# Decoder block on one core: keys projected ahead of queries in the linear-only steps, first loads reordered, the last linear output and its neighbours moved in the hand-written order

## The chip, the cores and the metric

One core of a Trainium2 chip. The metric is the device time of the kernel in microseconds (us). It was run three times: 1145.2, 1141.48 and 1145.28 us, median 1145.2.

## The reference

The kernel computes one pre-norm decoder layer on x (32 sequences, 128 tokens, 256 features) in fp32, with 16 heads of 16 features:

```
x = x + linear_attention(layernorm(x))        # causal; phi(q), phi(k) with phi = elu + 1
x = x + cross_attention(layernorm(x), ctx)    # softmax attention on a given context
x = x + ffn(layernorm(x))                     # silu(W1 x) * (W2 x), gelu(H1 .), gelu(H2 .), W3
```

In the linear attention, the weight of key s for query t is phi(q_t) . phi(k_s) for s <= t, and the sum is divided by the sum of the weights. The feed-forward widths are 256 to 1024 to 1024 to 1024 to 256, with ternary weights and one scale for each output.

## The kernel before

**Stages.** The 32 sequences are handled as 16 pairs. A step m (`step`, L660) works on the linear attention of pair m ("a_" units) and on the cross attention of pair m - 3 ("b_" units). Steps 0 to 2 use the list `first` (L621), in which only a_ units and the preparation of the first b_ pairs run; steps 3 to 15 use `both`; steps 16 and 17 use `alone` (L646), in which the linear attention is finished but for the tail of pair 15; step 18 uses `last`, step 19 uses `rest`. Then eight blocks of four sequences go through the feed-forward network (L771).

**Order.** Each list is an order written out by hand. A unit issues its instructions on TensorE (PE), VectorE (DVE), ScalarE (ACT) and GpSimd (POOL), and each engine executes what it was given in the order of the lists. SyncE (SP) issues most loads. An engine that has to wait for an operand therefore holds up everything listed behind it on that engine.

**The units that matter.** `a_queries` (L473) projects queries on PE (L359), then `phi` (L457) takes exp (L463) and relu (L465) on ACT and combines them on DVE (L467) in place in the buffer e; `masked` (L377) then makes two parity-masked copies, `qa2`, on POOL (L381), which read e. `a_keys` (L470) does the same into a buffer of its own, `ka`, with no masked copies. The buffers e and r exist once (`bufs=1`, L460 and L461). Only pair 0 has a separate e for its queries. `a_scores` (L487) multiplies keys and masked queries on PE (L388) into the two score buffers and applies the causal mask on DVE (L494). `a_weighted` (L502, PE L404, ACT copy L412), `a_divide` (L505, PE transposes L419, DVE L423 to L428), `a_turn` (L508, PE L512, ACT L514) and `a_out` (L517, PE L367, DVE addition to x L519) follow. `a_norm` and `b_norm` (L445, L524) take statistics on DVE (L134 to L143), twelve small instructions of a Newton iteration on POOL (L146 to L149) and two normalising instructions on POOL (L339). PE's small outputs share four PSUM banks in rotation (`bank`, L328).

**Fills.** In the tail of the attention, feed-forward work of block 0 is put between attention units. The list `fills` (L682) holds eleven pieces: the transposed input, eight gates (two products of 4 matmuls each, L229) and the first two of eight gelu chunks (16 matmuls each, L239). The unit `beside` (L631) starts one fill on PE, `settle` (L638) issues what follows it on ACT, DVE and POOL, and then reloads the exp table (L83). Both do nothing until the last linear output, `(a_out, 15, 1)`, is issued (L668).

**First loads.** `load_w` (L282) loads one of seven 256 KB projection weights; L287 to L302 write out which queue issues which and in what order: 0 to 3 are the query, key, value and output weights of the linear attention, 4 to 6 the query, key and value weights of the cross attention.

Of the kernel before, what the change touches and what calls it, by code (L numbers as in the profile page):

```python
# [26 lines left out]
NPAIR = B // 2  # L27
# [19 lines left out]
def decoder_block_kernel(  # L47
# [14 lines left out]
    nc = tc.nc  # L62
# [19 lines left out]
    def load_exp():  # L82
        nc.scalar.activation(warm, zero, AF.Exp)  # L83
# [172 lines left out]
    def pool(stack, name, bufs, **kw):  # L256
        return stack.enter_context(tc.tile_pool(name=name, bufs=bufs, **kw))
# [4 lines left out]
    with tc.manual_schedule(engines=ORDERED):  # L262
# [15 lines left out]
        def load_x(count):  # L278
            for _, n in zip(range(count), loads):
                nc.sync.dma_start(out=xs[n], in_=x[2 * n : 2 * n + 2].rearrange("b s d -> s b d"))  # L280

        def load_w(queue, n):  # L282
            queue.dma_start(
                out=WA[:, n] if n < 4 else WB[:, n - 4], in_=wattn[n].rearrange("(c p) o -> p c o", p=P)
            )
# [2 lines left out]
        load_w(nc.scalar, 5)  # L288
        load_x(1)
        nc.sync.dma_start(out=cT0, in_=ctxT[:, : 2 * S].rearrange("(c p) t -> p c t", p=P))  # L290
        load_w(nc.scalar, 6)
        nc.scalar.dma_start(out=col, in_=cols)
        load_w(nc.sync, 0)
        load_w(nc.scalar, 1)
        load_exp()
        load_x(1)
        load_w(nc.sync, 2)
        nc.sync.dma_start(out=row, in_=rows.partition_broadcast(P))
        load_w(nc.sync, 3)
# [304 lines left out]
        def b_divide(m, j):  # L604
# [14 lines left out]
            (b_scores, 0, 1), (a_weighted, 0, 1), (a_out, 0, 0), (a_norm, 2), (a_values, 1), (b_load, 2),  # L619
        ]  # L620
        first = [  # L621
            (a_scores, 0, 0), (a_norm, 2), (a_turn, -1, 1), (a_queries, 1), (a_out, -1, 1), (b_norm, 2),
            (a_weighted, 0, 0), (a_bias, 0), (a_scores, 0, 1), (a_divide, 0, 0), (a_keys, 1),
            (b_transpose, 1), (a_values, 1), (a_weighted, 0, 1), (a_turn, 0, 0), (a_bias, 1),
            (b_queries, 1), (a_transpose, 2), (a_out, 0, 0), (a_divide, 0, 1), (b_load, 2),
        ]
# [11 lines left out]
        def settle():  # L638
# [4 lines left out]
                load_exp()  # L643
            begun.clear()

        alone = [  # L646
            (b_load, 2), (b_maxima, 0, 0), settle, (b_weighted, -1, 1), (a_divide, -1, 1), (b_transpose, 1),
            (b_values, 1), (b_turn_maxima, 0, 0), (b_divide, -1, 1), (a_turn, -1, 1),
            (b_queries, 1), (b_scores, 0, 0), (a_out, -1, 1), beside, (b_norm, 2),
            (b_maxima, 0, 1), settle, (b_weighted, 0, 0), beside,  # L650
            (b_turn_maxima, 0, 1), (b_divide, 0, 0), settle, (b_keys, 1), (b_scores, 0, 1), beside,
        ]
        last = [
            (b_maxima, 0, 0), settle, (b_weighted, -1, 1), beside, (b_turn_maxima, 0, 0), (b_divide, -1, 1),
            settle, (b_scores, 0, 0), beside, (b_maxima, 0, 1), settle, (b_weighted, 0, 0), beside,
            (b_turn_maxima, 0, 1), (b_divide, 0, 0), settle, (b_scores, 0, 1), beside,
        ]
        rest = [(b_weighted, -1, 1), settle, beside, (b_divide, -1, 1), settle]

        def step(m):  # L660
            b = m - SKEW
            units = (
                first if m < prologue else both if m < NPAIR
                else alone if b < NPAIR - 1 else last if b < NPAIR else rest
            )
            for unit in units:
                if unit in (beside, settle):
                    if (a_out, NPAIR - 1, 1) in done:  # L668
                        unit()
                    continue  # L670
                f, ahead, *j = unit
                n = ahead + (b if f.__name__.startswith("b_") else m)
                if 0 <= n < NPAIR and (f, n, *j) not in done:
                    done.add((f, n, *j))
                    f(n, *j)
                    if (f, n, *j) == (a_out, NPAIR - 1, 1):
                        right.close()
                        hid["r"] = pool(ffn, "hr", 1, side="right", reuse_waits="tile")
# [7 lines left out]
        done = {(a_norm, 0), (a_norm, 1), (a_transpose, 1)}  # L686
# [21 lines left out]
        for m in range(NPAIR + SKEW + 1):  # L708
            waiting = None
            if m >= prologue and spare:  # L710
                n = spare.pop(0)
                dst = (W1, W2, H1)[FFN_SLICES[n][0]]
                load(n, dst)
                waiting = again(lambda: stages.tile([P, TB], F32, tag="stage", name="stage"), n)
            step(m)
            if waiting:
                test(dst, *waiting)
            if m == NPAIR - 1:
                block["xn"] = ffn_norm(0, nc.gpsimd)
# [217 lines left out]
```

## Time and profile before

| what | value |
|---|---|
| three runs | 1145.2, 1141.48, 1145.28 us |
| the profiled execution | 1142.26 us, of which the span from the first to the last instruction is 1140.2 us |
| granted TensorE clock, mean | 0.993 |
| start and step 0 (0 to 35.1 us) | PE busy 27.5 us of 35.1 |
| step 1 (35.1 to 52.85 us) | PE busy 15.3 us of 17.75 |
| step 2 (52.85 to 70.9 us) | PE busy 17.3 us of 18.05 |
| step 3 (70.9 to 99.5 us) | PE busy 28.2 us of 28.6 |
| step 16 with its fills and the start of step 17 (447.1 to 471.8 us) | PE busy 22.3 us of 24.7 |
| 471.8 us to 503.0 us | PE busy 30.0 us of 31.2 |

Starts are in us from the beginning of the span. A row of the timeline gives start, length, engine, line, operation, output and inputs, the count, and in brackets how long the engine was idle before it and what ended that wait. In the windows view each row gives the busy time of each engine in a stretch and the TensorE clock that was granted; 1.00 is full and 0.50 half.

### The profile page before, as it was taken

How to read it: one execution, taken by the hardware profiler on the slowest of the kernel's cores; microseconds unless marked ns; L12 is line 12 of the kernel's file. 1: busy time of each engine (PE TensorE's matmuls, PEld its weight loads, DVE VectorE, ACT ScalarE, POOL GpSimd, SP SyncE). 2: the span in 40 equal slices, each digit the busy share in tenths (PEclk: the TensorE clock that was granted, in tenths of full speed). 3: DMA queues.
4: the chain of work that ended last, by engine and by line, in shares of the span. 5: the costliest groups of instructions: out<-in, count | busy, mean ns of one | idle time of the engine just before them, and what ended most of it. 6: DMA issues, size and time to landing. Idle time of an engine off the chain costs nothing.

```text
span 1140.2 us, 20344 instructions
## 1 busy us (share of the span) xinstructions
PE 1118.8 (98%) x8238; PEld 904.3 (79%) x8238; DVE 576.7 (51%) x1296; ACT 411.9 (36%) x655; POOL 446.9 (39%) x1025
## 2 busy tenths in 40 slices
PE   8899999999999998999999999999999999999998
PEld 6677777777777776778888888888888888888887
DVE  6567777777777777452243443432522522522411
ACT  3344444444444444882231221321311311312311
POOL 4455555555555545455231231321311411412311
PEclk9899999999999999999999999999999999999999
DMA  8001111111111100005001111000000000000000
GB/s 273 1 20 48 48 47 48 48 47 48 47 48 48 47 11 11 1 2 185 17 22 37 38 38 37 19 14 5 24 10 5 19 1 1 20 1 10 9 1 22
DMA packets 26548, 39.28 MB, mean 34 GB/s; under 512 B 2512, under 2 KB 18640, under 8 KB 26448
## 3 DMA queue, kind: packets, MB, share of 16 engines
q1 hardware_dynamic: 21456, 25.57, 6.6%
q0 software_dynamic: 4032, 11.54, 3.1%
q8 instruction: 67, 1.10, 0.4%
q10 hardware_dynamic: 960, 0.81, 0.2%
q14 instruction: 33, 0.27, 0.1%
HBM read 33.71 MB, written 4.19 MB: 33 GB/s over the span
## 4 chain that ended last, share of the span: by engine, by line
PE 92%; DVE 3%; ACT 2%; POOL 1%; issue 1%; DMA 0%; SPq 0%; POOLq 0%; DVEq 0%
PE ph L218 50%; PE pp L359 9%; PE py L757 5%; PE pf L404 5%; PE pv L367 4%; PE se L388 3%; PE sa L388 3%; PE pw L367 3%; PE sm L388 3%; PE po L419 3%; PE pt L349 1%; DVE at L494 1%; PE se L588 1%; DVE nm L565 1%; PE pz L574 1%
## 5 line engine op out<-in xcount | busy, mean ns | idle before, releaser
L181 DVE TENSOR_TENSOR gl<-hg,gh 128x512 fp32r<-128x512 f32 x126 | 87.2, 692 | 347.0 <-POOL gh L180 344.0
L180 POOL CAST gh<-hg 128x512 fp32r<-128x512 f32 x128 | 79.1, 618 | 362.4 <-ACT hg L242 362.4
L242 ACT ACTIVATE hg<-ph,col 128x512 f32<-128x512 f32 x128 | 88.3, 690 | 363.0 <-PE ph L218 363.0
L218 PE MATMUL ph<-sh,H 128*128 128x512 f32 x512 | 199.5, 390 | 0.0
L218 PE MATMUL ph<-sl,H 128*128 128x512 f32 x512 | 199.2, 389 | 0.0
L218 PE MATMUL ph<-gh,H 128*128 128x512 f32 x512 | 199.2, 389 | 0.0
L218 PE MATMUL ph<-gl,H 128*128 128x512 f32 x512 | 199.2, 389 | 0.0
L218 PEld LDWEIGHTS ph<-sh,H 128*128 128x128 f32 x512 | 96.1, 188 | 20.4 <-issue 0.5
L218 PEld LDWEIGHTS ph<-gl,H 128*128 128x128 f32 x512 | 96.1, 188 | 19.9
L218 PEld LDWEIGHTS ph<-gh,H 128*128 128x128 f32 x512 | 96.1, 188 | 19.9
L218 PEld LDWEIGHTS ph<-sl,H 128*128 128x128 f32 x512 | 96.1, 188 | 19.9
L218 PE MATMUL ph<-xh,W 128*128 128x512 f32 x256 | 100.6, 393 | 0.0
L218 PE MATMUL ph<-xl,W 128*128 128x512 f32 x256 | 99.8, 390 | 0.0
L180 POOL CAST sh<-hs 128x512 fp32r<-128x512 f32 x64 | 58.5, 914 | 68.8 <-DVE hs L234 60.4
L565 DVE TENSOR_REDUCE nm<-sm 128x8 f32<-128x1024 f32 x64 | 75.2, 1216 | 16.9 <-PE sm L388 16.9
L494 DVE TENSOR_TENSOR at<-sa,causal 128x1024 f32<-128x1024 f32 x64 | 75.2, 1215 | 6.2 <-PE sa L388 6.1
L232 ACT ACTIVATE sil<-ph,col 128x512 f32<-128x512 f32 x64 | 44.1, 690 | 74.9 <-PE ph L218 74.8
L146 POOL TENSOR_TENSOR t<-rstd 128x2 f32<-128x2 f32 x138 | 32.5, 236 | 90.8 <-DVE hv L143 83.6
L234 DVE SCALAR_TENSOR_TENSOR hs<-ph,col,sil 128x512 f32<-128x512 f32 x64 | 48.0, 750 | 36.4 <-PE ph L218 20.2
L598 ACT ACTIVATE pr<-se 128x1024 f32<-128x1024 f32 x64 | 62.0, 1022 | 12.0 <-PE se L588 11.9
L757 PE MATMUL py<-W,gh 128*128 128x256 f32 x256 | 62.6, 285 | 0.0
L757 PE MATMUL py<-W,gl 128*128 128x256 f32 x256 | 62.0, 283 | 0.0
(133 smaller groups left out, 1937.7 us busy)
## 6 DMA issues: line engine op xcount, KB each, us to landing
x<-in_x_dram SPq DMA_DIRECT2D x16, 256.0 KB, 5.5
cT<-in_ctxT_dram SPq DMA_DIRECT2D x16, 256.0 KB, 2.6
stage<-in_h1T_dram SPq DMA_DIRECT2D x16, 256.0 KB, 2.9
H<-in_h1T_dram POOLq DMA_DIRECT2D x8, 512.0 KB, 3.6
H<-in_h2T_dram POOLq DMA_DIRECT2D x8, 512.0 KB, 7.1
out_dram<-y SPq DMA_DIRECT2D x32, 128.0 KB, 1.7
raw<-in_h2T_dram SPq DMA_DIRECT2D x16, 256.0 KB, 2.7
stage<-in_w1T_dram SPq DMA_DIRECT2D x4, 256.0 KB, 4.2
```

What stands on the lines that cost most here:

```text
L180: (high_engine.copy if high_engine is nc.scalar else high_engine.tensor_copy)(high, t)
L181: lows.append(lambda: low_engine.tensor_tensor(low, t, high.bitcast(F32), ALU.subtract))
L218: nc.tensor.matmul(pp, lhsT=w[:, k, ts(c, P)], rhs=parts[p], start=(k == 0 and p == 0), stop=(k == len(src) - 1 and p == 1),)
L242: nc.scalar.activation(t, pp, AF.Gelu, scale=col[:, c_scale + c : c_scale + c + 1])
L359: nc.tensor.matmul(pp[:, c, :], lhsT=w[:, d, ts(c, P)], rhs=src[:, d, :], start=(d == 0), stop=(d == DC - 1))
L367: nc.tensor.matmul(pp, lhsT=src[:, d, :], rhs=w[:, d, :], start=(d == 0), stop=(d == DC - 1))
L388: nc.tensor.matmul(sc[g // 2][:, g % 2, 2 * c : 2 * c + 2, :], lhsT=loaded[32 * g : 32 * g + 32, c, ts(j, S)], rhs=streamed[32 * g : 32 * ...
L404: nc.tensor.matmul(pf[32 * g : 32 * g + 32, i, :], lhsT=v[:, 4 * i + g, :], rhs=weights[g // 2][:, g % 2, i, :], start=True, stop=True,)
L494: nc.vector.tensor_tensor(at.rearrange("p g i s -> p (g i) s"), sc[u].rearrange("p g i s -> p (g i) s"), causal.unsqueeze(1).to_broadcast( ...
L565: nc.vector.tensor_reduce(nm[:, 2 * u : 2 * u + 2, :], sc[u], AX.X, ALU.max, negate=True)
L598: nc.scalar.activation(pr, sc[u], AF.Exp)
L757: nc.tensor.matmul(py[:, :D], lhsT=h[k][p][:, ts(j, S)], rhs=W3[:, k, :], start=(k == 0 and p == 0), stop=(k == HC - 1 and p == 1),)
```

## The change

Three things are moved, and no arithmetic is added or removed.

1. First loads: weight 6 (cross values) and weight 1 (linear keys) are issued by SP instead of ACT, weight 1 after the second x tile.
2. In `first`, `a_keys` of the next pair takes the place of `a_queries` and the other way round.
3. Step 16 has a list of its own, `begins`, in which the last `a_turn` and `a_out` come ahead of `b_queries`, and there is one more `beside` after `b_scores`. `alone`, now for step 17 only, loses the units that do nothing there. The test that kept fills back until the last linear output is dropped, because the list itself now puts it first. With the additional place in step 16, the eleven fills are used up in step 18, and the place in `rest` finds none.

```diff
         load_w(nc.scalar, 5)
         load_x(1)
         nc.sync.dma_start(out=cT0, in_=ctxT[:, : 2 * S].rearrange("(c p) t -> p c t", p=P))
-        load_w(nc.scalar, 6)
+        load_w(nc.sync, 6)
         nc.scalar.dma_start(out=col, in_=cols)
         load_w(nc.sync, 0)
-        load_w(nc.scalar, 1)
         load_exp()
         load_x(1)
+        load_w(nc.sync, 1)
         load_w(nc.sync, 2)
...
         first = [
-            (a_scores, 0, 0), (a_norm, 2), (a_turn, -1, 1), (a_queries, 1), (a_out, -1, 1), (b_norm, 2),
-            (a_weighted, 0, 0), (a_bias, 0), (a_scores, 0, 1), (a_divide, 0, 0), (a_keys, 1),
+            (a_scores, 0, 0), (a_norm, 2), (a_turn, -1, 1), (a_keys, 1), (a_out, -1, 1), (b_norm, 2),
+            (a_weighted, 0, 0), (a_bias, 0), (a_scores, 0, 1), (a_divide, 0, 0), (a_queries, 1),
             (b_transpose, 1), (a_values, 1), (a_weighted, 0, 1), (a_turn, 0, 0), (a_bias, 1),
             (b_queries, 1), (a_transpose, 2), (a_out, 0, 0), (a_divide, 0, 1), (b_load, 2),
         ]
...
+        begins = [
+            (b_load, 2), (b_maxima, 0, 0), (b_weighted, -1, 1), (a_divide, -1, 1), (b_transpose, 1),
+            (b_values, 1), (b_turn_maxima, 0, 0), (a_turn, -1, 1), (b_divide, -1, 1), (a_out, -1, 1), beside,
+            (b_queries, 1), (b_scores, 0, 0), beside,
+            (b_norm, 2), (b_maxima, 0, 1), settle, (b_weighted, 0, 0), beside,
+            (b_turn_maxima, 0, 1), (b_divide, 0, 0), settle, (b_keys, 1), (b_scores, 0, 1), beside,
+        ]
         alone = [
-            (b_load, 2), (b_maxima, 0, 0), settle, (b_weighted, -1, 1), (a_divide, -1, 1), (b_transpose, 1),
-            (b_values, 1), (b_turn_maxima, 0, 0), (b_divide, -1, 1), (a_turn, -1, 1),
-            (b_queries, 1), (b_scores, 0, 0), (a_out, -1, 1), beside, (b_norm, 2),
+            (b_maxima, 0, 0), settle, (b_weighted, -1, 1), (b_transpose, 1), (b_values, 1),
+            (b_turn_maxima, 0, 0), (b_divide, -1, 1), (b_queries, 1), (b_scores, 0, 0), beside,
             (b_maxima, 0, 1), settle, (b_weighted, 0, 0), beside,
             (b_turn_maxima, 0, 1), (b_divide, 0, 0), settle, (b_keys, 1), (b_scores, 0, 1), beside,
         ]
...
-                else alone if b < NPAIR - 1 else last if b < NPAIR else rest
+                else begins if m == NPAIR else alone if b < NPAIR - 1 else last if b < NPAIR else rest
             )
             for unit in units:
                 if unit in (beside, settle):
-                    if (a_out, NPAIR - 1, 1) in done:
-                        unit()
+                    unit()
                     continue
```

## The prediction

> **What bounds the kernel now.** I read the page first: its busy times, and the row of the granted clock.
>
> ```profile
> PE 1118.8 (98%) x8238; PEld 904.3 (79%) x8238; DVE 576.7 (51%) x1296; ACT 411.9 (36%) x655; POOL 446.9 (39%) x1025
> ...
> PEclk9899999999999999999999999999999999999999
> ```
>
> PE is busy for 1118.8 of 1140.2 us, and no matmul is added or removed. So the change can only win from PE's 21 us of idle time and from stretches at a reduced clock: slice 2 (28.5 to 57 us) has the one 8 in the row of the clock, and a shorter stretch, too short for this row, appears below at 455.6 us. Both lie in edited steps. Next the waits of the whole run:
>
> ```profile
> ACT e L463 <- POOL qa L381: 17.2, 3, 6.2
> ...
> PE pt L349 <- ACT r L465: 3.9, 2, 2.1
> PE pz L574 <- DVE z L570: 2.3, 2, 2.0
> ```
>
> Three times, once in each linear-only step, ACT stands before the exp of the keys until POOL has read e for the masked queries: e exists once. The timeline of step 0 shows what this does to PE:
>
> ```profile
> 27.59 1.35 POOL L381 TENSOR_SCALAR qa<-e,col 128x512 f32<-128x512 f32 x2
> 28.19 0.44 PE L512 MATMUL pot<-ident,oa 128*128 128x128 f32 x2
> 28.98 0.84 ACT L463 ACTIVATE e<-pp,col 128x256 f32<-128x256 f32 x2 [6.22 <-POOL qa L381]
> 30.70 0.63 PE L349 MATMUL pt<-ident,xna 128*128 128x128 f32 x4 [2.07 <-ACT r L465]
> 32.26 2.05 PE L367 MATMUL pw<-WA,oT 128*128 128x256 f32 x4 [0.94 <-ACT xTa L351]
> 35.09 1.33 PE L388 MATMUL sa<-qa,ka 32*128 32x256 f32 x16
> ```
>
> The masks run at 27.59, behind Newton and xna on POOL; exp and relu of the keys end at 30.55; only then is the PSUM bank free that PE's transposes need. PE loses 2.07 + 0.94 us here, 1.80 + 0.68 in step 1, 0.15 + 0.54 in step 2: 6.2 us. Then the windows view, cut where the clock changes:
>
> ```profile
> 28.93:32.35 3.42, 0.72 (x5) 0.54 (x5) 1.57 (x2) 2.91 (x7) 3.21 (x5) 0.96 0.00 0
> 32.35:35.76 3.41, 3.41 (x16) 2.59 (x20) 0.92 (x4) 0.00 (x0) 0.00 (x0) 0.54 0.00 0
> 46.00:49.42 3.42, 1.54 (x26) 0.87 (x18) 0.92 (x3) 2.37 (x7) 2.84 (x9) 0.96 0.00 0
> 49.42:52.83 3.41, 2.81 (x8) 2.06 (x8) 0.87 (x2) 0.54 (x1) 2.96 (x9) 0.50 0.00 0
> 52.83:56.24 3.41, 3.41 (x22) 2.48 (x22) 2.12 (x5) 0.37 (x1) 0.49 (x1) 0.54 0.02 5
> 452.20:455.60 3.40, 1.70 (x9) 1.39 (x10) 2.81 (x7) 1.43 (x2) 2.74 (x10) 0.96 0.00 0
> 455.60:459.00 3.40, 3.40 (x26) 2.31 (x24) 0.26 (x1) 1.21 (x3) 2.23 (x3) 0.53 0.02 5
> ```
>
> PE's busy time is the second column, the clock the third from the end. Each stretch of about 3.4 us with PE busy 0.72 to 1.70 us is followed by half clock, once for two stretches. That is 13.6 us at half clock, some 6 us of lost work. The last stall, in step 16:
>
> ```profile
> 450.61 2.35 DVE L565 TENSOR_REDUCE nm<-sm 128x8 f32<-128x1024 f32 x2
> 453.55 0.30 PE L574 MATMUL pz<-ident,z 128*128 128x128 f32 x1 [2.03 <-DVE z L570]
> ```
>
> **Part 1, the loads: 0 us.** SP takes over two issues of 0.46 us (ACT's two took 1.02), so x1 is issued about 0.5 us later. Its statistics began at 8.49, when DVE finished the Newton steps of x0; six transfers of 256 KB (1.5 MB) at the 310 GB/s of the first 17.4 us take 5.1 us, which is before that. Key weights have until 12.8 (second half of the 16 projections from 10.95). The wait of SP at 4.86 for the landing of weight 5 stays, the same transfer being still ninth. The gain is cT. [...] But by the order in which the data are needed, weight 6 no longer shares the engines with cT0: up to 256 KB, 0.8 us at 310 GB/s, off cT's landing (4.58 us after issue), for which PE waited 1.66 us. That would be the sum by the row of that wait. I take 0 nonetheless: the first transposes had to wait for POOL's xna at 9.78 (PE had ended the values at 9.64), and x0 still competes with weight 5 alone. Bounds: 0.1 us gained; 0.5 us lost if x1 were late.
>
> **Part 2, keys first.** Nothing is new but the order; PSUM banks rotate alike. Step 0 runs as before to 28.63 on PE (the projections at 18.49 and 23.63 only change names). DVE frees e and r with ka at 23.2; the exp of the queries no longer waits: 25.55, relu to 27.1 (1.55 for the four), DVE e 27.8, va 28.5. So the transposes start at 28.63 and end at 29.25; ACT copies fa to 28.9, oT to 29.3; pw 29.35 to 30.35, po to 30.9. On POOL, two bias additions (1.41) now come ahead of the masks (1.36): xna ends at 27.61, masks at 30.4. Scores of step 1: 30.9 against 35.09, a gain of 4.2 us (3.0 of idle, 1.2 of half clock).
>
> Step 1 has a new wait. The masks are now listed behind `b_norm`. POOL: DVE's statistics end 5.2 us after the scores start (17.41 to 22.64), at 36.1; Newton 3.8, xna 1.1, Newton 3.8, xnb 1.1, masks 1.36, with 0.3 of gaps: 47.6. PE meanwhile: scores 1.15, turn 0.4, keys 1.75, output 1.0, weighted 1.0, scores 1.1, divide 0.5, queries 1.75, values 1.75 to 41.3 (DVE's mask at(1,1) ends there too), weighted 1.05, turn 0.4, transposes 0.5, then 0.4 until va frees a bank, output 1.0, divide 0.55: 45.2. PE then waits 2.4 us for qa; all that is queued behind these scores waits with it. Scores of step 2 at 47.6 against 52.85: 5.2 us gained in all. If the 11.5 us of POOL work from 36.1 were shorter by a fifth, the stall would be 0.1, if longer by a fifth 4.7.
>
> Step 2 took 18.06 us before, with 0.69 of idle and 1.7 of half clock; without both 15.7. Masks of pair 3 end near 64.2, needed at about 66.8 behind `b_maxima`, transposes and `b_values`: covered by 2.6 us. Step 3 would start at 63.4 against 70.9: 7.5 us.
>
> The clock decides the rest. [...] The rows above show half clock behind stretches that were still busy for half of their 3.4 us. They are the nearer evidence: 2.4 us of idle in one stretch brings one at half clock, 1.7 us. I take 5.8 us; both ends, 4.1 (two such stretches) and 7.5, stay in the range.
>
> **Part 3, step 16.** Turn, oT copy (0.37) and output go ahead of `b_queries`; PE waits about 0.3 for oT. Output and the eight transposes end near 444.3, queries 446.0, scores 447.4. DVE's x, xh's lows xl end near 446.6, ahead of gate 0 (447.4 to 449.4). The maxima follow at 449.4, as ACT's exp frees their banks, to 450.7; nm at 450.8, z 453.6, hs 454.4. Between stand weighted (1.0) and gate 1 (2.1), to 453.75; then pz waits 0.7 for a bank that hs frees, keys 0.3 for ACT's silu. Step 17's maxima end at 462.2, before at 462.8, with one more gate done (2.0 us): worth 2.6 us, which is the 2.03 + 0.35 stall and the half clock (1.7), less 1.3 of new waits.
>
> What it costs later: step 18 now ends with gates 6, 7 and both gelu chunks. Gate 7 has the place of gate 6, whose hs came at 496.45; sh takes 0.61 and sl 1.28 on POOL, to 499.2. Gelu 0 starts at 494.3 and wants sl after 15 of 16 matmuls, 3.45 us, at 497.75: 1.5 us of stall. In `rest` nothing stands between weighted and divide: fb's copy (0.59 plus about 0.1) is bare, 0.7 us; before, gelu 1 covered it. Relative to the old times, the feed-forward chunk 2 starts at 507.2 against 508.12, a gain of 0.9 us. Bounds: a half-clock stretch behind the 1.5 us (-0.8), or sl in time (+2.4).
>
> **Sum.** 5.8 + 0.9 = 6.7 off the profiled 1142.26: 1135.6. The median of the runs is 2.9 above the profiled run; two of three lay there. I forecast 1136.5, between 1135.6 and 1138.5. A measurement of this kernel tells about 0.5%, 5.7 us, from no change.
>
> **Rivals.** (a) As summed: 1136.5, chance 0.47. (b) The full clock holds: 7.5 + 0.9 to 2.4: 1133, chance 0.13. (c) The gain is given back: two half-clock stretches behind the qa wait and one behind gelu 0, 4.1 - 0.8 = 3.3 off 1142.3 to 1145.2: 1140.5, chance 0.24. For it: 49.42 to 56.24 shows two in a row. (d) POOL, not e, is what holds the prologue (it is busy 3.21 of 3.42 us at 28.93), and reordering does nothing: 1142, chance 0.06. Against it: exp starts within 0.03 us of the masks' end. (e) Slower: the masks, put behind `b_norm` on POOL, arrive a full Newton and xnb later (4.95 us) at the scores of both steps 2 and 3, bare, and only step 0's 3.0 us is saved: 1142.3 + 9.9 - 3.0 = 1149, chance 0.10. It decides once the masks end over 8 us behind PE's arrival in the two steps together; I find 2.4 and none.
>
> Faster by over 0.5%: (a) and (b), 0.60; within: 0.29; slower: 0.11. Range 1131 to 1143.5, leaving out (e) and the edges.
>
> **What would show it.** Right: no ACT wait of e for qa; in step 1 a wait of PE's sa for POOL of 2 to 3 us; step 3's maxima near 64 to 65; no 2.03 us at pz; a stall of ph at gelu 0. Wrong: a sa stall above 5 us, another half-clock pair, or first projections later than 5.95.

## The result

| | median | lowest to highest |
|---|---|---|
| before, six runs | 1143.97 us | 1140.87 to 1145.28 |
| changed, six runs | 1136.3 us | 1134.37 to 1138.04 |

The ratio is 0.9938, 95% interval 0.9919 to 0.9957: 7.1 us are gained. The changed kernel's profiled execution took 1138.04 us, the slowest of the six, with a span of 1136.2 us. So the two traces differ by only 4.0 us (1140.2 before), and have to say where the rest of the gain is.

### The profile page after: what moved, and what is told of

Read it like the earlier page. It is cut to its first block, busy times and chain, and to the rows that moved or that the text cites. A ratio compares the mean times of both kernels' runs of the same rounds, so it can differ in the third digit from the quotient of the medians.

```text
span 1136.2 us, 20345 instructions
## 1 busy us (share of the span) xinstructions
PE 1117.1 (98%) x8238; PEld 902.7 (79%) x8238; DVE 577.3 (51%) x1296; ACT 411.4 (36%) x655; POOL 446.8 (39%) x1025
## 4 chain that ended last, share of the span: by engine, by line
PE 88%; DVE 3%; POOL 3%; ACT 2%; issue 2%; DMA 1%; SPq 0%; POOLq 0%; DVEq 0%; ACTq 0%
PE ph L218 47%; PE pp L359 9%; PE py L762 5%; PE pf L404 5%; PE pv L367 4%; PE se L388 3%; PE sa L388 3%; PE sm L388 3%; PE pw L367 3%; PE po L419 2%; PE pt L349 1%; DMA H<-in_h2T_dram 1%; DVE at L494 1%; PE se L588 1%; DVE nm L565 1%
## 5 line engine op out<-in xcount | busy, mean ns | idle before, releaser
L359 PE MATMUL pp<-xTa,WA 128*128 128x256 f32 x256 | 62.2, 388 | 0.7 <-ACT xTa L351 0.7
```

Of the source, the lines that this page charges most:

```text
L359: nc.tensor.matmul(pp[:, c, :], lhsT=w[:, d, ts(c, P)], rhs=src[:, d, :], start=(d == 0), stop=(d == DC - 1))
```

## The profile after

The page of the changed kernel, its busy times and the row of the granted clock:

```profile
PE 1117.1 (98%) x8238; PEld 902.7 (79%) x8238; DVE 577.3 (51%) x1296; ACT 411.4 (36%) x655; POOL 446.8 (39%) x1025
...
PEclk9999999999999999999999999999999999999999
```

The work is the same, and the 8 in slice 2 is gone. PE's own waits, of the same kernel (total, times, longest):

```profile
PE sa L388 <- POOL qa L381: 2.8, 1, 2.8
...
PE ph L218 <- POOL sl L181: 0.8, 1, 0.8
...
PE po L419 <- ACT fb L412: 0.7, 1, 0.7
```

All three are new, and all three were in the working: qa before the scores of step 2, sl at gelu 0, and fb in the last step. The wait of ACT's exp for qa is nowhere in the list. The timeline of step 0, changed kernel:

```profile
26.93 0.84 ACT L463 ACTIVATE e<-pp,col 128x256 f32<-128x256 f32 x2 [2.80 <-PE pp L359]
29.83 0.60 PE L349 MATMUL pt<-ident,xna 128*128 128x128 f32 x4
30.61 1.13 PE L367 MATMUL pw<-WA,oT 128*128 128x256 f32 x4 [0.17 <-ACT oT L514]
30.85 1.35 POOL L381 TENSOR_SCALAR qa<-e,col 128x512 f32<-128x512 f32 x2
32.26 1.15 PE L388 MATMUL sa<-qa,ka 32*128 32x256 f32 x16
```

The second exp now starts as soon as PE has its projection, and the transposes follow with no wait. Step 1 shows the price, on POOL and then on PE:

```profile
46.37 1.09 POOL L339 TENSOR_SCALAR xnb<-x,nmean,rstd 128x256 f32<-128x256 f32 x2
47.44 1.35 POOL L381 TENSOR_SCALAR qa<-e,col 128x512 f32<-128x512 f32 x2
48.85 1.15 PE L388 MATMUL sa<-qa,ka 32*128 32x256 f32 x16 [2.79 <-POOL qa L381]
```

Cut into parts at the same PE instructions, the two profiled spans compare so:

| part | before | after | difference |
|---|---|---|---|
| start of the span to the scores of step 0 | 17.41 | 18.78 | +1.37 |
| to the scores of step 1 | 17.68 | 13.48 | -4.20 |
| to the scores of step 2 | 17.76 | 16.59 | -1.17 |
| to the maxima of step 3 | 18.06 | 17.55 | -0.51 |
| to the first maxima of step 16 | 365.11 | 365.12 | 0 |
| to the last divide | 71.74 | 69.94 | -1.80 |
| to the transposes of feed-forward block 1 | 55.10 | 56.62 | +1.52 |
| to the end | 577.30 | 578.07 | +0.77 |

The 4.0 us are thus 5.9 from the linear-only steps and 1.8 from steps 16 to 19, less 3.7 in three parts (the start, block 0 and the end) of which the working had said nothing. Step 3's maxima came at 66.4, not near 64 to 65, because of the first of these.

The start is not the loads' doing in the way I had feared. First PE rows of before, then of the changed kernel:

```profile
5.95 1.97 PE L359 MATMUL pp<-cT,WB 128*128 128x256 f32 x8 [1.66 <-DMA cT<-in_ctxT_dram]
...
10.95 3.72 PE L359 MATMUL pp<-xTa,WA 128*128 128x256 f32 x16 [0.67 <-ACT xTa L351]
```

```profile
5.67 3.75 PE L359 MATMUL pp<-cT,WB 128*128 128x256 f32 x8 [1.38 <-DMA cT<-in_ctxT_dram]
...
12.32 3.72 PE L359 MATMUL pp<-xTa,WA 128*128 128x256 f32 x16 [0.73 <-ACT xTa L351]
```

cT came 0.28 us sooner, but the same eight matmuls took 3.75 us instead of 1.97: the array was at half rate. The granted-clock record opens with full clock at 4.8 us in before and at 9.3 us here.

## The experiments

My theory: the single e buffer holds ACT and through it PE; removing that wait brings nearly all of the gain; step 16 brings a little and the loads nothing. The main rival: the loads and step 16 pay, and the reordering only moves a wait from e to POOL. Each kernel was run beside the kernel before; ratios are to that (medians of before 1142.4 to 1143.3 us in these comparisons).

| kernel | median us | ratio, 95% interval |
|---|---|---|
| keys_alone | 1137.67 | 0.9956 [0.9941, 0.9971] |
| begins_alone | 1141.24 | 0.9988 [0.9980, 0.9996] |
| loads_alone | 1141.88 | 1.0001 [0.9988, 1.0013] |
| keys_in_place | 1133.53 | 0.9920 [0.9905, 0.9935] |
| after_again (the changed kernel) | 1135.81 | 0.9939 [0.9925, 0.9953] |
| bnorm_later | 1132.5 | 0.9903 [0.9886, 0.9920] |
| newton_on_dve | 1135.96 | 0.9934 [0.9917, 0.9951] |
| no_extra_place | 1137.58 | 0.9954 [0.9939, 0.9969] |
| longer_warm_up | 1135.45 | 0.9933 [0.9919, 0.9947] |
| best_of_parts | 1131.36 | 0.9907 [0.9894, 0.9921] |

**One part at a time.** keys_alone is the kernel before with the change of `first`:

```diff
-            ... (a_turn, -1, 1), (a_queries, 1), (a_out, -1, 1), (b_norm, 2),
-            ... (a_divide, 0, 0), (a_keys, 1),
+            ... (a_turn, -1, 1), (a_keys, 1), (a_out, -1, 1), (b_norm, 2),
+            ... (a_divide, 0, 0), (a_queries, 1),
```

> The kernel before with keys ahead of queries in the linear-only steps and nothing else. Theory (the single e buffer held ACT, and through it PE): about 5.9 us below before, near 1138; no wait of ACT's exp for qa; scores of step 1 about 13.5 us after those of step 0 (17.7 before); a new wait of about 2.8 us of step 2's scores for qa and a stretch at half clock behind it. Rival (the loads and the new order of step 16 brought the time, and the reordering only moved a wait): within 2 us of before.

Measured: 5.0 us gained by the ratio, interval 3.3 to 6.7. Its trace has the qa wait of 2.8 us of PE's scores, and from step 0's scores to those of step 1 it takes 13.5 us, as expected. The expected half clock behind that wait did not come: the clock is 1.00 from 39.42 to 63.31 us. The rival that the reordering pays nothing has fallen.

begins_alone is the kernel before with the list `begins`, the shortened `alone` and the test for the last output removed, and with the old loads and old `first`.

> The kernel before with the new list for step 16 and nothing else. Theory: the 2.0 us wait of pz is gone, step 16 to the first feed-forward chunk of the layer loop is 1.8 us shorter, and 1.5 us come back in block 0, where GpSimd issues the last weights late: 0 to 1 us below before, about 1143.5. Rival (the step-16 part is what pays): 3 us or more below before.

Measured: 1.4 us gained by the ratio, interval 0.5 to 2.3. The pz wait is gone; the part to the last divide takes 69.9 us (71.7 before, with a stretch at clock 0.50 in it, 455.35 to 458.76 us). Block 0 returned only 0.3 us of it (55.4 against 55.1), not 1.5.

loads_alone is the kernel before with the two moved loads.

> The kernel before with the two weight loads moved from ScalarE's queue to SyncE's and nothing else. Theory: cT lands about 0.3 us sooner, and nothing follows, since xna of pair 0 is ready no sooner: within 0.5 us of before, 1144. Rival (SyncE's longer list delays x1 or the key weights): slower by 0.5 us or more, with a DMA wait of DVE or PE in the first 15 us. Rival (cT's landing was the limit): faster by 0.3 us or more.

Measured: no difference. PE waited for cT 1.3 us instead of 1.7, and step 0's scores did not come sooner: 19.40 us, with first projections at half rate (3.75 us against 1.97). Nothing in it waits for x1 or for the key weights. The three parts together give 0.9956 x 0.9988 x 1.0001 = 0.9945, and the changed kernel gave 0.9938 and, again, 0.9939: they add up within the intervals.

> The changed kernel itself, beside the three that vary it. By the parts measured alone (keys 4.8 to 5.0 us, step 16 1.3 to 1.4, loads none) it should be 6.2 us below before; the first comparison had 0.9938, 7.1 us.

**Is e the wait?** keys_in_place leaves the order of before as it was and takes the shared buffer away:

```diff
         def a_keys(m):
-            A[m]["k"] = phi(project(WK, A[m]["xT"]), C_BK, "ka")
+            k = buffer([P, DC, 2 * S], F32, tag="ka", name="ka")
+            A[m]["k"] = phi(project(WK, A[m]["xT"]), C_BK, e=k)
```

> The kernel before, queries still first, but phi of the keys computed in place in ka, so that the keys' exp no longer shares e with the queries. Theory (e is the wait, and the masks behind b_norm are the price of the reordering): the exp no longer waits for qa, and qa is masked ahead of b_norm, so that step 2's scores wait for nothing: 8 to 10 us below before, about 1135, faster than keys_alone by 2 to 4 us. Rival (POOL's own length is what holds these steps): no better than keys_alone.

Measured: 9.1 us gained by the ratio, 4.1 more than keys_alone. Its timeline in step 0:

```profile
27.76 0.84 ACT L463 ACTIVATE ka<-pp,col 128x256 f32<-128x256 f32 x2 [2.80 <-PE pp L359]
...
30.30 1.35 POOL L381 TENSOR_SCALAR qa<-e,col 128x512 f32<-128x512 f32 x2
30.66 0.60 PE L349 MATMUL pt<-ident,xna 128*128 128x128 f32 x4
32.94 1.15 PE L388 MATMUL sa<-qa,ka 32*128 32x256 f32 x16
```

The keys' exp starts 2.5 us ahead of the masks. So e was what held ACT, and POOL's length was not; with queries first, their masks also stay ahead of `b_norm`, and step 2's scores wait for nothing.

**Is the qa wait the masks' place behind `b_norm`?** bnorm_later is the changed kernel with a list of its own for step 1:

```diff
+        later = [unit for unit in first if unit != (b_norm, 2)]
+        later.insert(later.index((a_values, 1)) + 1, (b_norm, 2))
...
-                first if m < prologue else both if m < NPAIR
+                later if m == 1 else first if m < prologue else both if m < NPAIR
```

> The changed kernel with b_norm of step 1 listed behind a_values, so that the masks of qa come ahead of it on POOL. Theory (the 2.8 us wait of step 2's scores is the masks' place behind b_norm, and the half clock follows from it): the wait goes, the half-clock stretch goes with it, 3.5 to 4.5 us below the changed kernel. Rival (the statistics of b_norm, now later on DVE, delay va or the next mask as much): within 1 us of it.

Measured: 3.3 us below the changed kernel by medians (0.9903 against 0.9939). The rows answer to those of step 1 above:

```profile
43.56 1.36 POOL L381 TENSOR_SCALAR qa<-e,col 128x512 f32<-128x512 f32 x2 [0.74 <-DVE e L467]
46.20 0.74 PEld L388 LDWEIGHTS sa<-qa,ka 32*128 32x128 f32 x16 [0.17 <-POOL t L147]
46.20 1.15 PE L388 MATMUL sa<-qa,ka 32*128 32x256 f32 x16
49.06 1.10 POOL L339 TENSOR_SCALAR xnb<-x,nmean,rstd 128x256 f32<-128x256 f32 x2
```

The masks are done 1.3 us before the scores, and no PE wait for xnb, now 2.7 us later than in the changed kernel, is in its trace. The rival that the wait would move elsewhere has fallen. The gain by medians is a little less than the 3.5 us expected; the half clock that I had counted in it was not in the trace of after_again either (1.00 from 37.67 to 61.56 us).

**The loss in block 0.** newton_on_dve gives the last pair's Newton steps to DVE:

```diff
-                pair_stats(m, nmean3[...], rstd3[...])
+                pair_stats(m, nmean3[...], rstd3[...], engine=nc.vector if m == NPAIR - 1 else nc.gpsimd)
```

> The changed kernel with the Newton steps of pair 15's last statistics on DVE instead of POOL. In block 0 the changed kernel lost 1.5 us against before, with PE waiting for gl. Theory (POOL starts to issue the last weights only when these Newton steps are done, 9.4 us after the first layer-loop chunk against 8.2 before, and its casts wait among those issues): the issues start 3 to 4 us sooner and 1 to 1.5 us come back. Rival (the loads wait for their own landings whatever the start): nothing comes back.

POOL's first issue of the last weights, in the changed kernel and then here:

```profile
511.29 1.70 POOL L107 DMA_DIRECT2D H<-in_h2T_dram  x3 [0.62 <-issue]
```

```profile
505.49 1.71 POOL L107 DMA_DIRECT2D H<-in_h2T_dram  x3
```

From the last divide (501.46 and 500.86) that is 9.8 us against 4.6, and the block takes 55.15 us where the changed kernel took 56.62. But in after_again it took 55.48, in begins_alone 55.41, with the first issue 9.8 us behind the last divide as well; so the usual loss is 0.3 us, of which DVE wins all back, and the further 1.1 us were seen in one execution only. The time shows no difference (1135.96 against 1135.81). My expectation of 1 to 1.5 us was wrong.

**The additional fill place.** no_extra_place takes one `beside` out of `begins`:

```diff
-            (b_queries, 1), (b_scores, 0, 0), beside,
+            (b_queries, 1), (b_scores, 0, 0),
```

> The changed kernel without the additional fill place behind the first scores of step 16; the last linear output stays early, and the second gelu chunk returns to the last step. Theory (the output's place alone frees nothing, since PE then waits 1.5 to 2 us for ACT's exp to free the score banks and again for the maxima; the extra gate fills that, and its price is 0.8 us at gelu 0, 0.7 us in the last step and 1.5 us in block 0): those three waits vanish, a wait of some 2 us or more in step 16 is back, and the time is within 1.5 us of the changed kernel. Rival (the early output alone pays): 2.5 to 3 us below the changed kernel.

Measured: 1137.58 us, 1.8 us above the changed kernel by medians, with intervals that overlap; I had expected it within 1.5 us. In its trace the 0.8 at gelu 0 and the 0.7 of the last step are gone, and PE waits in step 16 instead:

```profile
442.32 0.70 PE L388 MATMUL sm<-kb,qb 32*128 32x256 f32 x4 [1.17 <-ACT pr L598]
443.24 1.13 PE L388 MATMUL sm<-kb,qb 32*128 32x256 f32 x12 [0.21 <-ACT pr L598]
...
448.32 1.99 PE L359 MATMUL pp<-cT,WB 128*128 128x256 f32 x8 [0.35 <-DVE mT L576]
```

In this trace, its fastest run (1134.55), the part to the last divide takes 70.22 us against 69.94: the place itself is worth 0.3 us there. Block 0 gives that back: without the place POOL's first issue comes 8.6 us behind the last divide instead of 9.8, and the block takes 55.09 us, as before. So in the traces the place wins nothing, and the 1.8 us by medians have no explanation. The ten runs spread up to 1141.5; what the slower ones lost, no trace shows. The early output alone does not win the 2.5 us that the rival wanted.

**The start.** longer_warm_up is the changed kernel with 18 idle transposes instead of 12.

> The changed kernel with 18 idle transposes at the start instead of 12. The traces so far differ at the start: step 0's scores began at 17.41 us where full clock was granted from 5.0 us, and at 18.6 to 20.2 where it came at 9 to 12 us. Theory (PE stands idle from 4.3 us to the first projections near 5.8, and the stretch of 3.4 us that holds this gap does not count as busy): with PE busy up to 5.7 us full clock comes by 8.3 us, step 0's scores begin by 18.3, and 0.5 to 1.5 us are gained on the changed kernel. Rival (the onset does not depend on that gap): no gain, and up to 0.3 us lost if the transposes reach past cT's landing.

Its first PE rows:

```profile
1.47 4.10 PE L700 MATMUL idle<-ident 128*128 128x128 f32 x18 [1.47 <-POOL ident masks.py:199]
6.00 2.30 PE L359 MATMUL pp<-cT,WB 128*128 128x256 f32 x8 [0.43 <-DMA cT<-in_ctxT_dram]
...
17.65 1.15 PE L388 MATMUL sa<-qa,ka 32*128 32x256 f32 x16 [0.58 <-DVE ka L467]
```

The eight projections from cT took 2.30 us (3.75 in the changed kernel), and step 0's scores came at 17.65; in the traces with 12 transposes they came at 18.6 to 20.2 us, but for before's own 17.41. The start is about 1 us or more better in the trace than in those others; the time is 0.4 us below the changed kernel by medians, which these intervals can't tell from nothing. This one had the half clock behind the qa wait: its scores of step 2 took 2.09 us, against 1.15 in the changed kernel.

**Together.** best_of_parts has queries first with phi of the keys in place, the new loads and step 16, the last Newton steps on DVE and 18 transposes.

> Queries first again, with phi of the keys in place in ka; the new loads and the new step 16 as in the changed kernel; the last Newton steps on DVE; 18 idle transposes. If the parts add up: keys_in_place 9.1 below before, step 16 1.3, the warm-up about 1, DVE's Newton 0.3: 11 to 12 us below before, 0.990, faster than bnorm_later (0.9903). If they overlap (full clock in the prologue already taken): 9 to 10 us below before.

1131.36 us is the lowest median of all, 11 us under that of before beside it, but its ratio 0.9907 (10.6 us) is no better than that of bnorm_later (0.9903), and only 1.5 us better than that of keys_in_place, with overlapping intervals. In its trace step 3's maxima come at 60.7 us (66.4 in the changed kernel). So bnorm_later and best_of_parts both beat the two kernels, and which of them is faster is not settled.

## Why the prediction was right, and where it was not

**Total.** 1136.5 was forecast and 1136.3 measured, a gain of 7.1 (by the ratio) to 7.7 us (by the medians) against the 6.7 of the sum. Part of that is luck. In the profiled pair, parts 2 and 3 gave 7.7 us and terms that the sum left out took 3.7 back. In the other traces those terms are smaller or have nothing to do with the change (see below), and four of six had the full clock for which the sum had allowed only in part.

**The loads, 0 us: right.** loads_alone showed no difference. Whether weight 6 shared cT's time is not shown: with 12 idle transposes, PE waited for cT 1.3 to 1.6 us in the six traces with the new loads and 1.4 to 1.9 us in the four with the old ones. The ranges overlap, and what lies between them is less than my bound of 0.8.

**Keys first, step by step: right.** Scores of step 1 4.2 us sooner (4.2 forecast). Scores of step 2 5.4 us sooner, counted from those of step 0 (5.2 forecast), with a wait of 2.79 us (2.4). Step 2's masks at 63.8 to 65.2 were covered, as worked out.

**The clock: half right.** I took it that 2.4 us of idle brings a stretch at half clock. The windows view of the changed kernel, cut at the recorded changes of the clock:

```profile
43.45:46.86 3.41, 2.43 (x18) 1.80 (x14) 1.87 (x6) 1.36 (x3) 2.56 (x11) 1.00 0.02 5
46.86:50.27 3.41, 1.42 (x19) 1.07 (x20) 0.39 (x2) 0.00 (x0) 3.30 (x6) 1.00 0.00 0
50.27:53.69 3.42, 3.42 (x10) 2.70 (x10) 3.32 (x8) 0.37 (x1) 0.00 (x0) 0.50 0.00 0
```

(The cuts in the prediction lie 0.25 us behind these changes, hence its clocks of 0.96 and 0.54. Cut at the changes, its three stretches were busy for 0.63, 1.61 and 1.45 us.) PE was busy for 1.42 of 3.41 us, and half clock followed. But of six traces with this same wait only two show half clock behind it (this one, 0.50, and longer_warm_up, 0.54 from 47.89 to 51.30 us). newton_on_dve does not:

```profile
45.05:48.47 3.42, 1.67 (x9) 1.18 (x8) 1.27 (x5) 0.73 (x2) 2.73 (x11) 1.00 0.02 5
48.47:51.88 3.41, 2.16 (x22) 1.74 (x23) 0.98 (x1) 0.37 (x1) 2.57 (x4) 1.00 0.00 0
```

The wait is 2.8 us long in both. Here a stretch's end divides it, 1.57 us before and 1.25 behind; in the changed kernel 1.99 us of it lay in one stretch. The changes of the clock lie at 4.79, 32.10, 35.51, 49.16, 55.99, 455.35 and 458.76 us in before and at 9.31, 50.27 and 53.69 us in the changed kernel (those at the end of the run aside), whole multiples of 3.413 us apart in each. Half clock came in before behind stretches with PE busy for 0.63, 1.61 and 1.45 us, and here behind 1.42 us. In stretches cut up to 0.3 us behind the changes, it came behind 1.11 us in loads_alone (48.46 to 51.87 us) and 0.61 us in longer_warm_up (44.48 to 47.89 us). Full clock came in newton_on_dve behind the 1.67 and 2.16 us above, in after_again behind 1.89 and 1.97 us (cut at 44.50, 47.91 and 51.32 us), and in no_extra_place behind 1.94 and 1.92 us (cut at 44.13, 47.55 and 50.96 us). One case does not fit: in keys_alone PE was busy for 1.25 us of the stretch with this wait (46.24 to 49.66 us), and the clock stayed at 1.00; why stays open.

From step 0's scores to step 3's maxima the traces of the new order without half clock take 45.9 us, with it 47.3 to 47.6, and the kernel before 53.5. So the 7.5 us of case (b) were there in four of six, against before's own trace. That trace is the worst of its order: begins_alone and loads_alone, with the old order as well, took 51.9 and 52.8 us.

**Step 16: right in kind, its size too small.** 0.9 us net was forecast, though the terms listed for it (2.6 less 1.5 and 0.7) come to 0.4; 1.8 us came in the part to the last divide, as the waits that PE shows in step 16 are 0.19 and 0.27 us instead of 1.3 in all, and gelu 0 waited 0.8 instead of 1.5. fb's wait of 0.7 us was met. keys_alone, which keeps the old step 16, took 70.4 us for the part, and the eight projections behind its 2.0 us wait took 1.99 us; in before they took 3.12 us, and the clock was 0.50 from 455.35 to 458.76 us. So without the half clock the new order is worth 0.5 us, and the other 1.3 us are what before's trace lost to the clock. keys_in_place met the slow projections again: 3.65 us, from 447.24 us.

**What the working missed.** The state of the clock at the start (1.4 us), block 0 behind POOL's later issues (0.3 to 0.4 us in begins_alone and after_again, 1.5 here), and 0.8 us between the last addition and the end of the span. That last stretch takes 4.3 to 4.4 us in four traces and 5.0 to 5.5 in eight, and bnorm_later and no_extra_place, which have the changed kernel's end, are among the four; so it is not the change that lengthens it. Before's own profiled start was a fortunate one, and its half clock in three places (from 32.10, 49.16 and 455.35 us) unfortunate, so that a sum against it could be off by 2 us either way.

## What to carry to other kernels

If a buffer that exists once makes one engine wait for another, look first for a place where the result can be made in place: that cost nothing and gave 9.1 us, where reordering gave 5.0 and a new wait. When two units change places, list for every engine what the moved instructions are now queued behind; the qa wait could be read off the list to 0.4 us. And split a gain from a removed stall into the idle time and the clock it costs, because the second comes and goes between executions: behind the 2.8 us wait two of six traces had it.

## What the runs showed of the hardware

The clock at the start was not the same in all traces. The same eight projections took 1.97 us in before and 3.75 in the changed kernel. The stretches that tell the two apart, before and then changed (ahead of its first record the clock column says 1.00, whatever the rate):

```profile
1.38:4.79 3.41, 2.82 (x12) 2.42 (x12) 2.77 (x3) 1.49 (x2) 2.52 (x9) 1.00 0.87 229
```

```profile
2.49:5.90 3.41, 2.03 (x10) 1.66 (x9) 2.92 (x9) 0.78 (x2) 1.41 (x4) 1.00 1.00 337
5.90:9.31 3.41, 3.41 (x9) 2.70 (x10) 2.96 (x18) 0.00 (x0) 0.83 (x2) 1.00 1.09 341
```

In before all 2.82 us of the 12 idle transposes fell into one stretch, and full clock followed at 4.79 us. In the changed kernel PE was busy for 2.03 us of the one and 3.41 us of the next, and full clock followed at 9.31 us. In the nine traces with 12 transposes other than before's, the changed kernel's among them, the eight projections took 3.55 to 3.75 us. With 18 transposes, and a gap of 0.43 us or less behind them, they took 2.30 us in longer_warm_up and 2.75 us in best_of_parts.

The way back from half clock, in before: behind the stretch from 49.16 to 52.58 us, with PE busy for 2.74 us, the clock stayed at 0.50 for another; behind those with PE busy for 3.25 us (32.10 to 35.51) and 3.41 us (52.58 to 55.99 and 455.35 to 458.76) it was 1.00.
